# A graph layer and a mixture of experts on one core: quarter slots for an expert's last rows, and columns of A loaded by half blocks

## The chip, the cores and the metric

The kernel runs on one core of a Trainium2 chip. The metric is the device time of one execution in microseconds; the time of a kernel is the median of its runs. One further execution is recorded by the hardware profiler, and all views come from that one.

## What is computed

There are 2048 nodes of 256 features. The layer norm of the rows is gathered over 67,584 weighted edges and summed into the destination rows, with the input and a node vector added. The result `x` goes through a mixture of eight experts: each row is sent to its two best ones.

```python
x = x + gnn(layernorm(x), edge_weight, [src, dst], node_vec1)   # segment sum of w * x[dst] over src
xt = layernorm(x)
logits = xt @ Wr + br                         # Wr: 256 x 8
top_p, top_idx = top_k(softmax(logits), 2);  weights = top_p / sum(top_p)
xn = layernorm(xt);  xe = xn * ln_g[e] + ln_b[e]
h = gelu(xe @ W1[e] + b1[e])                  # 256 x 1024
y = h @ W2[e] + b2[e]                         # 1024 x 256
out = x + sum over the row's two experts of weight * y
```

Everything is float32. 4096 pairs of row and expert have to be computed, about 512 for each expert.

## The kernel before

**Build of A.** The edge sums are matmuls with a dense matrix A (2048 x 2048), which is made on the chip from the sorted edge list. 32 half blocks `n` are made one after another; two of them give one block `cb` of 128 columns. `make_hots` makes one-hot matrices on VectorE (L306, L311, L318), the third part of `hr` on POOL; `make_cols` multiplies them on TensorE with four tiles of 32 columns side by side (L343), ScalarE copies the result to `ar` (L346), SP stores `ar` to `ad` in DRAM (L347) and, after the second half of a block, loads the whole block back as `ac`, in another layout (L350). `dense` (L357) multiplies finished blocks with the normalised rows, VectorE adds the products to `acc` (L364, L367). The last group of four blocks is multiplied after the build.

**Routing.** From `acc` come the second norm, the logits and the two best experts of each row, in two batches (ten blocks of rows, then six). `places` and `enlist` give each pair a spot in its expert's list; the list is kept in tiles of 128. `slots` (L858 to L908) turns the counts into a plan on VectorE: how many whole slots (two tiles, 256 rows) and half slots (one tile, 128 rows) each expert has, and where each slot starts. After it `set_shares` computes the weights of the pairs and SP stores the rows to `xr_d` (L774); SP then reads the plan into registers (L1134) and loads weights.

**Slots.** `load_slot` loads an expert's weights (L932 to L935, 2 MB, on SP) and gathers its rows by index on POOL (L939), into one of seven sets of buffers. `head` transposes the rows (L978), scales them (L987) and forms the weights; `layer_1` does 16 matmuls with gelu on ScalarE (L1013, L1015), `layer_2` 8 matmuls for each tile (L1027), VectorE weighs the result into `ys` (L1030, two buffers), and POOL adds it to `y_d` in DRAM by index (`put_y`, L1035). Stores of one slot are declared free of order among themselves; a store waits for those of other slots.

Ten whole slots always run (three of them early, on the first batch). `halves[0]` and `halves[1]` are loaded at u = 4 and 5, the two final slots at u = 7 and 8. Then come two nests of Ifs on counts from the plan: further whole slots, and after them half slots, as many as there are; with this input four and two. At the end SP copies `y_d` to `out` (L1180) as soon as all stores have landed, while TensorE works on the two final slots; these gather what the copy has for their rows (`so_far`), add it to their bias, and write to `out` (`put_out`, L1048).

The order on TensorE, VectorE, ScalarE and SP is as written; only POOL's is chosen by the scheduler.

## Time and profile before

| what | us |
|---|---|
| median of 3 runs (501.56 to 506.0) | 503.91 |
| the profiled execution | 508.05 |
| its span, first to last instruction | 506.3 |
| TensorE busy | 459.8 (91%) |
| VectorE busy | 273.1 (54%) |
| matmuls of layer 1 (L1013), 576 records | 121.3 |
| matmuls of layer 2 (L1027), 544 records | 121.0 |
| matmuls of the edge sums (L357), 512 records | 126.3 |

A float32 matmul is two records. 576 records of layer 1 are 18 slots of 32; 544 of layer 2 are 34 tiles of 16. Busy times are unions of a group's spans. In lines of the timeline the columns are start, duration, engine, line, operation, tiles written and read, shapes and count, and in brackets the idle time before and what ended it. In the table by stage each engine has its busy microseconds, then come TensorE's granted clock (1.00 is full), the busy share of the DMA engines, and GB/s.

### The profile page before, as it was taken

The numbers are of one execution on the slowest core, as the hardware profiler recorded it, in microseconds if no ns is written. First come the engines' busy times: TensorE is split into PE (matmuls) and PEld (weight loads), VectorE is DVE, ScalarE is ACT, GpSimd is POOL, SyncE is SP. The second block draws the span as 40 slices with busy tenths as digits, with TensorE's granted clock in tenths as the row PEclk, the third lists the DMA queues.
The fourth block names the chain that finished last, engine by engine and source line by source line (L and its number), as shares of the span: only waits on it lengthen the run. The fifth ranks groups of instructions, "written<-read, shape, count | busy, mean of one in ns | idle before, by whom it ended". The sixth has DMA issues, their size and how long they took to land.

```text
span 506.3 us, 12113 instructions
## 1 busy us (share of the span) xinstructions
PE 459.8 (91%) x4996; PEld 394.4 (78%) x4996; DVE 273.1 (54%) x621; ACT 183.8 (36%) x422; POOL 192.7 (38%) x158
## 2 busy tenths in 40 slices
PE   4876599898979999899999899999999999999993
PEld 3775478687758878788888788888888888888882
DVE  7999999999969971317837232323232312212111
ACT  2478524144214210028483323332243433333320
POOL 3477655544533330000142444443452444322231
PEclk9575679899979999999999999999999999999998
DMA  6128678796777667953513997997999677226420
GB/s 214 53 76 246 203 223 269 230 236 186 203 216 221 210 178 239 344 189 105 179 54 84 303 333 214 361 356 210 334 360 309 169 210 210 36 40 204 140 92 31
DMA packets 84356, 102.15 MB, mean 202 GB/s; under 512 B 8240, under 2 KB 74656, under 8 KB 82176
## 3 DMA queue, kind: packets, MB, share of 16 engines
q1 hardware_dynamic: 74832, 86.26, 53.5%
q0 software_dynamic: 7984, 13.91, 11.9%
q10 hardware_dynamic: 1472, 1.06, 0.7%
q8 instruction: 44, 0.72, 0.6%
q14 instruction: 24, 0.20, 0.1%
HBM read 75.18 MB, written 28.14 MB: 204 GB/s over the span
## 4 chain that ended last, share of the span: by engine, by line
PE 35%; DMA 13%; issue 3%; DVE 1%; SPq 0%; ACT 0%; POOL 0%; POOLq 0%; DVEq 0%
PE py L1027 16%; PE ph L1013 15%; DMA xs<-xr_d,to_i 8%; DMA y_d<-ys,to_i 2%; DMA out<-y_d 2%; PE px L978 1%; PE px L834 1%; PE py L357 1%; DMA so_far<-out,to_i 1%; DMA out<-ys,to_i 0%; SPq L1180 0%; POOL out L1048 0%; POOLq L1209 0%; ACT L1015 0%; DVE pick L957 0%
## 5 line engine op out<-in xcount | busy, mean ns | idle before, releaser
L357 PE MATMUL py<-xn_sb,ac 128*128 128x264 f32 x512 | 126.3, 404 | 1.8 <-DVEq L569 1.4
L1013 PE MATMUL ph<-xeT,w 128*128 128x256 f32 (+1 forms) x576 | 121.3, 368 | 2.4 <-PEq L1167 1.7
L1027 PE MATMUL py<-w,hT 128*128 128x256 f32 x544 | 121.0, 379 | 0.0
L1013 PEld LDWEIGHTS ph<-xeT,w 128*128 128x128 f32 x576 | 104.4, 190 | 16.5 <-issue 3.0
L357 PEld LDWEIGHTS py<-xn_sb,ac 128*128 128x128 f32 x512 | 98.5, 197 | 21.7 <-issue 2.2
L1027 PEld LDWEIGHTS py<-w,hT 128*128 128x128 f32 x544 | 101.9, 190 | 12.9
L1015 ACT ACTIVATE hT<-ph,ec 128x256 f32<-128x256 f32 (+1 forms) x144 | 66.2, 462 | 117.6 <-PE ph L1013 60.8
L1035 POOL DMA_INDIRECT y_d<-ys,to_i x30 | 48.5, 1616 | 119.3 <-DVE ys L1030 88.5
L318 POOL TENSOR_TENSOR hr<-eq,w 128x1024 bf16<-128x1024 bf16 x32 | 61.2, 1912 | 81.6 <-DVE hr L318 66.1
L343 PE MATMUL pa<-hl,hr 128*32 128x128 bf16 x3072 | 58.4, 237 | 21.6 <-POOL hr L318 10.8
L343 PEld LDWEIGHTS <-hr 128*32 128x32 bf16 x3072 | 50.0, 106 | 32.6 <-issue 14.0
L306 DVE TENSOR_TENSOR hl<-k,iota_t 128x4096 bf16<-128x4096 bf16 x32 | 72.9, 2278 | 0.0
L987 DVE TENSOR_SCALAR xeT<-px,ec 128x256 f32<-128x256 f32 (+1 forms) x38 | 18.4, 526 | 79.8 <-PE px L978 79.0
L939 POOL DMA_INDIRECT xs<-xr_d,to_i x39 | 40.5, 1038 | 54.2 <-DVE z L702 41.9
L346 ACT COPY ar<-pa 128x512 f32<-128x512 f32 x64 | 36.5, 584 | 59.8 <-PE pa L343 53.6
L1030 DVE SCALAR_TENSOR_TENSOR ys<-py,wt,b2w 128x256 f32<-128x256 f32 x34 | 16.4, 484 | 72.7 <-PE py L1027 61.3
L364 DVE TENSOR_TENSOR acc<-acc,py 128x528 f32<-128x528 f32 x32 | 22.3, 701 | 35.3 <-PE py L357 35.3
L318 DVE TENSOR_TENSOR hr<-eq,w 128x2048 bf16<-128x2048 bf16 x32 | 39.1, 1223 | 0.6
L1002 ACT ACTIVATE b2w<-b,wt 128x256 f32<-128x256 f32 x36 | 16.3, 500 | 34.0 <-DVE wt L1000 32.4
L311 DVE TENSOR_TENSOR eq<-k,iota_t 128x1024 bf16<-128x1024 bf16 x32 | 21.8, 680 | 0.0
L670 ACT ACTIVATE sq<-acc,less_m 128x256 f32<-128x256 f32 x16 | 8.0, 499 | 32.6 <-DVE acc L364 32.6
L296 ACT CAST w<-r 128x256 bf16<-128x256 f32 x16 | 6.5, 405 | 25.0 <-DVE r L295 25.0
(196 smaller groups left out, 303.0 us busy)
## 6 DMA issues: line engine op xcount, KB each, us to landing
w<-in_L_ffn_W SPq DMA_DIRECT2D x40, 1024.0 KB, 9.2
ad<-ar SPq DMA_DIRECT2D x32, 512.0 KB, 8.7
ac<-ad SPq DMA_DIRECT2D x16, 1024.0 KB, 5.9
b<-in_L_ffn_b SPq DMA_DIRECT2D x20, 128.0 KB, 9.8
out<-y_d SPq DMA_DIRECT2D x4, 512.0 KB, 6.3
xr_d<-rec SPq DMA_DIRECT2D x1, 1300.0 KB
y_d<-acc SPq DMA_DIRECT2D x1, 1280.0 KB, 5.1
acc<-in_x SPq DMA_DIRECT2D x2, 512.0 KB, 7.6
```

The costliest lines, as they stand in the source:

```text
L306: nc.vector.tensor_tensor(hl.rearrange("p g (n t) -> p g n t", t=2), two(k2[:, 0], g, P), pair(P), OP.is_equal)
L311: nc.vector.tensor_tensor(eq.rearrange("p g (n t) -> p g n t", t=2), two(k2[:, 1], g, RK), pair(RK), OP.is_equal)
L318: return engine.tensor_tensor(hr[:, i0:i1].rearrange("p i g (n t) -> p (i g) n t", t=2), eq[:, None, :, :].to_broadcast([P, i1 - i0, GH, RK]),
L343: nc.tensor.matmul(pa[j * RK:(j + 1) * RK, m, :], hr[:, i, g, :], hl[:, g, :], start=(i == 0), stop=(i == 2), tile_position=(0, j * RK))
L346: nc.scalar.copy(ar[:, m0:m0 + 4, :], pa)
L357: nc.tensor.matmul(pa[:, i, :DX], acs[c][:, b + i, :], xn_sb[:, c, :], start=(c == cbs[0]), stop=(c == cbs[-1]))
L364: nc.vector.tensor_add(acc[:, b:b + 2, :], acc[:, b:b + 2, :], pa[:, :, :DX])
L939: nc.gpsimd.indirect_dma_start(out=(sets[s.set][0] if into is None else into)[:, t, :], out_offset=None, in_=(xr_d if rows is None else ro ...
L1013: nc.tensor.matmul(ph, w1[:, k, c * P:(c + 1) * P], xeT[:, k, :], start=(k == 0), stop=(k == KD - 1))
L1015: nc.scalar.activation(hT[:, c, :s.n * P], ph, AF.Gelu, bias=ec[:, c:c + 1], scale=1.0)
L1027: nc.tensor.matmul(py, hT[:, c, t * P:(t + 1) * P], w2[:, c, :], start=(c == 0), stop=(c == KH - 1))
L1035: st = nc.gpsimd.indirect_dma_start(out=y_d[:, :], out_offset=bass.IndirectOffsetOnAxis(ap=tos[s.to][:, t:t + 1], axis=0), in_=ys, in_offs ...
```

## The change

An expert with an odd number of tiles whose last tile holds 1 to 32 rows no longer gets a half slot for it: up to two such experts get a quarter slot, run inside the loop of the whole slots. `few_e` and `few_t` hold its expert and tile, found in `slots`. In a quarter slot the 32 rows are the stationary operand, and the hidden units are split over four column tiles of 32; `fold` (32 columns out of a fourfold identity) sums the four partial results. Its five steps `turn`, `first`, `turn_h`, `second` and `total` are hung between matmuls of the slots u = 7 to 9. The quarter slots always run; without such an expert they work on spare rows. The half slots that remain run ahead of the conditional whole slots, and `halves[0]` is no longer loaded early. In the build, each half block gets its own buffer `ad` in DRAM and is loaded back by itself, after the store of the next half block has been issued.

```diff
@@ -83,6 +83,10 @@
+    NQ, QR = 2, 32
+    QW = P // QR
...
@@ -144,7 +148,10 @@
     tile_0 = consts.tile([P, TT, NU], F32, name="tile_0")
-    slot_i = consts.tile([1, NU + 2], I32, name="slot_i")
+    slot_i = consts.tile([1, NU + 2 + NQ], I32, name="slot_i")
+    few_e = consts.tile([P, NQ], F32, name="few_e")
+    few_t = consts.tile([P, NQ], F32, name="few_t")
+    fold = consts.tile([P, QR], F32, name="fold")
     xr_d = dram.tile([N + TS, RW], F32, name="xr_d")
...
@@ -329,10 +336,8 @@
-        cb, h = n // 2, n % 2
-        if h == 0:
-            ads[cb] = dram.tile([P, NB, P], F32, name="ad", bufs=4)
-        ad_v = ads[cb].rearrange("(m j) b r -> (j b) m r", m=GB // QP)
+        ads[n] = dram.tile([P // 2, NB, P], F32, name="ad", bufs=6)
+        ad_v = ads[n].rearrange("(m j) b r -> (j b) m r", m=GH // QP)
         ar = rowsp.tile([P, GH // QP, P], F32, name="ar")
...
@@ -344,10 +349,14 @@
             nc.scalar.copy(ar[:, m0:m0 + 4, :], pa)
-        nc.sync.dma_start(ad_v[:, h * GH // QP:(h + 1) * GH // QP, :], ar)
-        if h == 1:
-            acs[cb] = pool_of[cb].tile([P, NB, P], F32, name="ac")
-            nc.sync.dma_start(acs[cb], ads[cb])
+        nc.sync.dma_start(ad_v, ar)
+        for k in ([n - 1] if n > 0 else []) + ([n] if n == 2 * NB - 1 else []):
+            cb, h = k // 2, k % 2
+            if h == 0:
+                acs[cb] = pool_of[cb].tile([P, NB, P], F32, name="ac")
+            nc.sync.dma_start(acs[cb][h * P // 2:(h + 1) * P // 2], ads.pop(k))
...
@@ -657,8 +667,8 @@
     final = [Slot(FIRST - EARLY, TT, 3, AHEAD + 2, 2), Slot(FIRST - EARLY + 1, TT, 6, AHEAD + 6, 0)]
-    halves = [Slot(NF + i, 1, 4 + i if i < 2 else i % 3, AHEAD + 3 + i % 3, 3 + i % 2)
-              for i in range(NE)]
+    halves = [Slot(NF + i, 1, 4 + i % 2, AHEAD + 3 + i % 3, 3 + i % 2) for i in range(NE)]
+    few = [Slot(i, 1, 4 + i, AHEAD + 3 + i, 3 + i) for i in range(NQ)]
     with tc.manual_schedule(engines=ALL - {ET.Pool}):
...
@@ -858,10 +868,15 @@
             nc.vector.tensor_tensor(tiles_i, ps, over, OP.add)
+            few_i = small_t("few_i", I32)
+            nc.vector.tensor_scalar(few_i, tiles_i, QR.bit_length() - 1, None,
+                                    op0=OP.arith_shift_right)
+            nc.vector.tensor_scalar(few_i, few_i, TS // QR - 1, None, op0=OP.bitwise_and)
             nc.vector.tensor_scalar(tiles_i, tiles_i, 7, None, op0=OP.arith_shift_right)
...
@@ -873,6 +888,25 @@
                                            op1=OP.subtract)
+            is_few = small_t("is_few")
+            nc.vector.tensor_scalar(is_few, few_i, float(P // QR), None, op0=OP.is_equal)
+            n_few = small_t("n_few")
+            nc.vector.tensor_tensor_scan(n_few, ones[:, :NE], is_few, 0.0, op0=OP.mult, op1=OP.add)
+            last = small_t("last")
+            nc.vector.scalar_tensor_tensor(last, iota_p[:, :NE], float(NB), tiles[:, :NE],
+                                           op0=OP.mult, op1=OP.add)
+            for i in range(NQ):
+                it = small_t(f"few{i}")
+                nc.vector.scalar_tensor_tensor(it, n_few, float(i + 1), is_few, op0=OP.is_equal,
+                                               op1=OP.mult)
+                nc.vector.tensor_sub(n_of[:, 1, :], n_of[:, 1, :], it)
+                of_it = small_t(f"of_few{i}")
+                for t, v in ((few_e, iota_p[:, :NE]), (few_t, last)):
+                    nc.vector.scalar_tensor_tensor(of_it, it, 1.0, v, op0=OP.mult, op1=OP.mult,
+                                                   accum_out=t[:, i:i + 1])
+            nc.vector.tensor_scalar(few_t, few_t, -1.0, None, op0=OP.add)
+            nc.vector.tensor_copy(slot_i[:, NU + 2:], few_e[0:1, :])
             upto = route.tile([P, 2, NE], F32, name="upto", bufs=1)
...
@@ -894,7 +928,7 @@
             nc.vector.tensor_copy(slot_i[:, :NU], slot_e[0:1, :])
-            nc.vector.tensor_copy(slot_i[:, NU:], upto[0:1, :, NE - 1])
+            nc.vector.tensor_copy(slot_i[:, NU:NU + 2], upto[0:1, :, NE - 1])
             for i, r in spans:
...
@@ -1056,10 +1090,98 @@
-        def run_slot(s, nxt, more=(), between={}, put=put_y):
+        def load_few(s):
+            e = ds(few_offs[s.i], 1)
+            get_weights(s, W1[e], cols_d[e], W2[e], b2[e])
+            tk = slotp.tile([P, TT], F32, name="tk")[:QR, :1]
+            pick = slotp.tile([P, P], F32, name="pick", bufs=1)[:QR]
+            nc.vector.scalar_tensor_tensor(pick, iota_p[:QR], few_t[:QR, s.i:s.i + 1], lists[:QR],
+                                           op0=OP.is_equal, op1=OP.mult, accum_out=tk)
+            to = slotp.tile([P, TT], F32, name="to")[:QR, :1]
+            nc.vector.scalar_tensor_tensor(to, tk, 0.5, spare_r[:QR, :1], op0=OP.is_lt,
+                                           op1=OP.mult)
+            nc.vector.scalar_tensor_tensor(tos[s.to][:QR, :1], tk, -1.0, to, op0=OP.add,
+                                           op1=OP.max)
+            nc.gpsimd.indirect_dma_start(
+                out=sets[s.set][0][:QR, 0, :],
+                out_offset=None,
+                in_=xr_d[:, :],
+                in_offset=bass.IndirectOffsetOnAxis(ap=tos[s.to][:QR, :1], axis=0),
+            )
+        def few_steps(s):
+            xs, w1, w2, ec, b2r = sets[s.set]
+            xeT, wt, b2w = (t[:QR] if i else t[:, :, :QR] for i, t in enumerate(heads[s.head]))
+            part = lambda j: slice(j * QR, (j + 1) * QR)
+            hs = more_w.tile([P, TS], F32, name=f"hs{s.i}")
+            hT = more_w.tile([P, TT, P], F32, name=f"hT{s.i}")
+            py = more_w.tile([P, D], F32, name=f"py{s.i}")
+            def turn():
+                pt = ps_x.tile([P, KD, TS], F32, name="px")
+                for k in range(KD):
+                    nc.tensor.transpose(pt[:, k, :QR], xs[:QR, 0, k * P:(k + 1) * P],
+                                        ident[:QR, :QR])
+                for k in range(KD):
+                    nc.vector.tensor_scalar(xeT[:, k, :], pt[:, k, :QR], ec[:, KH + k:KH + k + 1],
+                                            ec[:, KH + KD + k:KH + KD + k + 1],
+                                            op0=OP.mult, op1=OP.add)
+                mine = slotp.tile([P, TT, 2], F32, name="mine")[:QR, 0, :]
+                nc.vector.tensor_scalar(mine, xs[:QR, 0, D:D + 2], few_e[:QR, s.i:s.i + 1], None,
+                                        op0=OP.is_equal)
+                wr = slotp.tile([P, TT, 2], F32, name="wr")[:QR, 0, :]
+                nc.vector.tensor_mul(wr, mine, xs[:QR, 0, D + 2:D + 4])
+                nc.vector.tensor_reduce(wt, wr, AX.X, OP.add)
+                nc.scalar.activation(b2w[:, 0, :], b2r[:QR], AF.Copy, scale=wt)
+            def first():
+                ph = ps_h.tile([P, TS], F32, name="ph")
+                for k in range(KD):
+                    for j in range(QW):
+                        nc.tensor.matmul(ph[part(j), :], xeT[:, k, :],
+                                         w1[:, k, j * TS:(j + 1) * TS], start=(k == 0),
+                                         stop=(k == KD - 1), tile_position=(0, j * QR))
+                nc.vector.tensor_copy(hs, ph)
+            def turn_h():
+                pt = ps_h.tile([P, TS], F32, name="ph").rearrange("p (t r) -> p t r", t=TT)
+                for t in range(TT):
+                    nc.tensor.transpose(pt[:, t, :], hs[:, t * P:(t + 1) * P], ident)
+                each = lambda a: a.rearrange("p t (j r) -> p t j r", j=QW)
+                bias = ec[:, :KH].rearrange("p (j t) -> p t j", t=TT)[..., None]
+                nc.vector.tensor_tensor(each(hT), each(pt), bias.to_broadcast([P, TT, QW, QR]),
+                                        OP.add)
+                nc.scalar.activation(hT, hT, AF.Gelu)
+            def second():
+                pa = listed.rearrange("p a b -> p (a b)")
+                for t in range(TT):
+                    for j in range(QW):
+                        nc.tensor.matmul(pa[part(j), :], hT[:, t, part(j)], w2[:, j * TT + t, :],
+                                         start=(t == 0), stop=(t == TT - 1),
+                                         tile_position=(0, j * QR))
+                nc.vector.tensor_copy(py, pa)
+            def total():
+                pa = counts.rearrange("p a b e -> p (a b e)")[:QR, :D]
+                nc.tensor.matmul(pa, fold, py, start=True, stop=True)
+                ys = slotp.tile([P, D], F32, name="ys")[:QR]
+                nc.vector.scalar_tensor_tensor(ys, pa, wt, b2w[:, 0, :], op0=OP.mult, op1=OP.add)
+                nc.gpsimd.indirect_dma_start(
+                    out=y_d[:, :],
+                    out_offset=bass.IndirectOffsetOnAxis(ap=tos[s.to][:QR, :1], axis=0),
+                    in_=ys,
+                    in_offset=None,
+                    compute_op=OP.add,
+                )
+            return turn, first, turn_h, second, total
+        def run_slot(s, nxt, more=(), between={}, put=put_y, between_1={}):
             for m in more:
                 m()
-            hT = layer_1(s)
+            hT = layer_1(s, between_1)
             if nxt is not None:
...
@@ -1135,6 +1257,10 @@
         )
+        _, few_offs = nc.values_load_multi_w_load_instructions(
+            slot_i[0:1, NU + 2:], engines=[mybir.EngineType.SP], min_val=0, max_val=NE - 1,
+            skip_runtime_bounds_check_because="an expert's number, or none",
+        )
         load_slot(whole[EARLY])
...
@@ -1148,15 +1274,40 @@
             nc.vector.memset(t, 0.0)
+        nc.vector.tensor_reduce(fold, ident.rearrange("p (j r) -> p r j", r=QR), AX.X, OP.add)
         for u in range(3, FIRST):
             more = later(load_slot if u + 2 <= FIRST else load_rows, whole[u + 2])
-            more += later(load_slot, *{4: halves[:1], 5: halves[1:2], 7: final[:1], 8: final[1:]}.get(u, []))
-            also = {FIRST - 2: halves[0], FIRST - 1: final[0]}.get(u)
-            run_slot(whole[u], whole[u + 1], more, {1: lambda: head(also)} if also else {})
+            more += later(load_slot, *{7: final[:1], 8: final[1:]}.get(u, []))
+            more += later(load_few, *{4: few[:1], 5: few[1:]}.get(u, []))
+            f = u - (FIRST - 1 - NQ)
+            between, between_1 = {}, {}
+            if 0 <= f < NQ:
+                steps = few_steps(few[f])
+                between[1] = steps[0]
+            if 0 <= f - 1 < NQ:
+                between_1 = {1: ready[1], 5: ready[2]}
+                between[0] = ready[3]
+                between.setdefault(1, lambda: None)
+                t0, t1 = between[1], ready[4]
+                between[1] = lambda t0=t0, t1=t1: (t1(), t0())
+            if u == FIRST - 1:
+                t0 = between.get(1, lambda: None)
+                between[1] = lambda t0=t0: (t0(), head(final[0]))
+            run_slot(whole[u], whole[u + 1], more, between, between_1=between_1)
+            if 0 <= f < NQ:
+                ready = steps
     _, (n_whole, n_half) = nc.values_load_multi_w_load_instructions(
...
     )
+    with ExitStack() as nest:
+        for u, s in enumerate(halves):
+            nest.enter_context(tc.If(n_half > s.i - NF))
+            with tc.manual_schedule(engines=ALL - {ET.Pool}):
+                if u == 0:
+                    load_slot(s)
+                head(s)
+                run_slot(s, None, later(load_slot, *halves[u + 1:u + 2]))
     with ExitStack() as nest:
...
@@ -1164,14 +1315,6 @@
                          + later(load_rows, *whole[u + 2:u + 3]))
-    with ExitStack() as nest:
-        for u, s in enumerate(halves):
-            nest.enter_context(tc.If(n_half > s.i - NF))
-            with tc.manual_schedule(engines=ALL - {ET.Pool}):
-                if u >= 2:
-                    head(s)
-                run_slot(s, halves[1] if u == 0 else None,
-                         later(load_slot, *halves[u + 1:u + 2] * (u > 0)))
...
```

## The prediction

> **What bounds the kernel now.** First the totals and the table by stage, to see which engine has no slack where.
>
> ```profile
> PE 459.8 (91%) x4996; PEld 394.4 (78%) x4996; DVE 273.1 (54%) x621; ACT 183.8 (36%) x422; POOL 192.7 (38%) x158
> core 0: us, PE busy (x) PEld busy (x) DVE busy (x) ACT busy (x) POOL busy (x), PEclk, DMA share, GB/s
> 80.00:120.00 40.00, 37.83 (x871) 30.87 (x862) 39.04 (x60) 15.91 (x41) 19.83 (x14) 0.96 0.78 220
> 290.00:396.00 106.00, 106.00 (x510) 93.42 (x509) 31.22 (x125) 34.93 (x75) 44.75 (x35) 1.00 0.95 305
> 453.00:468.00 15.00, 14.53 (x98) 13.37 (x98) 2.74 (x12) 6.39 (x17) 4.21 (x3) 1.00 0.67 181
> ```
>
> Up to about 190 us, where the columns of A are built, VectorE is full (39.04 of 40 us); from 290 us TensorE is full (106.00 of 106 us). So in the build a microsecond counts if it is VectorE's, and among the slots if it is TensorE's. Then the timeline of TensorE at the end of the slots:
>
> ```profile
> 445.38 7.07 PE L1027 MATMUL py<-w,hT 128*128 128x256 f32 x32
> 453.03 3.83 PE L1013 MATMUL ph<-xeT,w 128*128 128x128 f32 x32 [0.57 <-PEq L1160]
> 456.91 3.62 PE L1027 MATMUL py<-w,hT 128*128 128x256 f32 x16
> 460.37 3.73 PE L1013 MATMUL ph<-xeT,w 128*128 128x128 f32 x32
> 463.94 3.62 PE L1027 MATMUL py<-w,hT 128*128 128x256 f32 x16
> 469.22 7.14 PE L1013 MATMUL ph<-xeT,w 128*128 128x256 f32 x32 [1.66 <-PEq L1167]
> ```
>
> Two half slots run between the last whole slot and the two final ones, with a gap of TensorE's sequencer at each branch out of a nest of Ifs. Working the reference's routing on its inputs gives the experts 544, 509, 506, 482, 502, 510, 536 and 507 rows: the half slots carry the last 32 and 24 rows of experts 0 and 6, both within the change's 32. Third, the one stall among the slots, from the timelines of VectorE, SP, POOL and TensorE:
>
> ```profile
> 268.28 0.16 DVE L864 TENSOR_TENSOR tiles_i<-counts,over 128x8 int32<-128x8 f32 x1
> 272.66 0.22 DVE L908 TENSOR_TENSOR tile<-tile,skipped 128x54 f32<-128x54 f32 x1
> 273.45 0.36 SPq L774 DMA_DIRECT2D xr_d<-rec  x1
> 280.14 1.03 POOL L939 DMA_INDIRECT xs<-xr_d,to_i  x1 [0.30 <-DVE to L961]
> 287.67 0.44 PE L978 MATMUL px<-ident,xs 128*128 128x128 f32 x2 [1.88 <-DMA xs<-xr_d,to_i]
> ```
>
> The planner `slots` (L864 to L908) stands on VectorE ahead of the shares, these ahead of the store of the rows, and that ahead of the gather for `whole[3]`. TensorE waits 1.88 us for that gather, so this chain has no slack.
>
> **What the Trainium skill says.** "TensorE: Matmul & The Clock Gate", Part 3 (Packing small matmuls), says matmuls in different column tiles run concurrently while matmuls still start in program order. The trace agrees: L343 starts in groups of four column tiles, and 96 of them take 1.46 us (166.58 to the next line's 168.04, below), 15 ns each. The same page, Part 1, says the clock halves after an idle window of about 3.4 us; here the table has clock 1.00 at 498 to 502 us, after the last matmul ended at 497.5, and 0.51 at 502 to 506. "Runtime: NRT & Kernel Launch", Instruction fetch mechanics, says a taken branch breaks sequential prefetch; the gaps of 0.57 and 1.66 us above agree in place.
>
> ```profile
> 166.58 1.52 PE L343 MATMUL pa<-hl,hr 128*32 128x128 bf16 x96
> 168.04 2.94 PE L357 MATMUL py<-xn_sb,ac 128*128 128x264 f32 x12
> 92.89 1.07 ACT L346 COPY ar<-pa 128x512 f32<-128x512 f32 x2 [1.45 <-DMA ad<-ar]
> 131.27 0.70 DVE L364 TENSOR_TENSOR acc<-acc,py 128x528 f32<-128x528 f32 x1 [0.80 <-PE py L357]
> ```
>
> **The change, part by part.** The sum is made against the profiled execution: 508.05 us, span 506.3. The median of the runs is 503.91; I carry the difference over to it.
>
> (a) The half slots go. The last whole slot's matmuls end at 452.45. Its branch gap of 0.57 stays, so the finals start at 453.02 instead of 469.22: 16.2 us less on TensorE. But the end also hangs on the last store to `y_d`, the copy to `out`, and the gathers of `so_far`. Before, that store was issued 1.53 us after the last matmul of the slots (467.56 to 469.09); after `whole[13]` it is 0.87 us (452.45 to 453.32). This chain had 0.65 us of slack against TensorE (`b2w` done at 496.33, first `ys` 0.5 us, second `ys` at 497.56). The last two POOL stores stand in series. So I take 15.8 off. The transposes of `halves[0]` at 377.08 go too: 0.2.
>
> (b) Two quarter slots come, on TensorE. Each issues two transposes of 32 rows (`turn`), 8 matmuls of 32 columns by 256 (`first`), two transposes (`turn_h`), 8 such matmuls (`second`) and one of 256 (`total`). A float32 matmul is two records: 32 records of 256 columns take 6.91 us, 216 ns each. Transposes: 4 in 0.44 us. The trace has no column-tiled float32. With no overlap, 8 matmuls take 16 x 0.216 = 3.46 us; with four side by side as at L343, 0.86 plus the 0.18 us that L343 lost against its ideal (estimate: 1.46 less 96 x 53.3 ns / 4, with the page's price of 128 columns), 1.04. But the two records of one matmul use the same column tile, and starts are in order: the second record waits 216 ns, and only the next tile's first record can go beside it. That gives 9 steps of 216 ns, 1.95 us, which I take. Each quarter: 0.12 + 1.95 + 0.22 + 1.95 + 0.43 = 4.7; with some draining 4.8. Two: +9.6 us (6.0 to 15.5).
>
> (c) `slots` gets 15 small VectorE instructions and four accumulator reads ahead of the store. The 13 instructions from 268.28 to 270.33 have a pitch of 0.158 us, dependent ones 0.20, and a read adds 0.12. 15 x 0.16 + 4 x 0.12 = 2.9 us. Beside it: `head(whole[2])` is ready at 278.6 instead of 275.7, when TensorE needs it at 278.50, so nearly free. SP's two more register loads delay the weights of `whole[3]` by 0.3 us more, hidden, since they were issued 16 us ahead of use. The gather moves by the whole amount. POOL may order it ahead of the store that now precedes it and win back 1.3 us. I take +2.7 (1.5 to 4; the upper end if a gap of now 4.6 us halves the clock for a while).
>
> (d) The nest of halves is now jumped over ahead of the conditional whole slots: one gap. Long cover in TensorE's queue gave 0.57, short cover 1.66. There is a layer's second half ahead of it: +0.6 (0 to 1.7). Of the other engines, VectorE has some 10 us to its next urgent work, ScalarE 5.3, and SP runs ahead.
>
> (e) The store of a quarter slot is not exempted from order with the other stores to `y_d`, which need 6.7 us in the median to land. POOL holds it behind the first store of its whole slot and holds the second store behind it. `ys` has two buffers, and a third user now comes in a slot: VectorE's second `ys` waits for the first store. In the slot after the first quarter this blocks VectorE until about 7.5 us after the first tile's matmuls. Picks (1.2 us) stand ahead of the copy of `hs`, done near 9.7. TensorE, with three `ph` buffers, wants that one back near 8.6: +1.2 us (0 to 4). Gathers behind POOL's stores have 10 us to spare.
>
> (f) Half-block loads. SP no longer sits behind a load that waits for its own store: it waited 102.9 us in all for `ad` at L350. What of this reaches VectorE? ScalarE waited three times for `ad` (2.63, 1.45, 1.25 us), delaying TensorE, and soon after VectorE idled 0.95, 0.61 and 0.80 us for `py`. At the first, TensorE also waited for `ac`, of which only half is now late. So -1.7 (-2.4 to +0.5, the latter for 16 more issues on SP). The last columns landed near 204 us and are needed at 209: no gain there.
>
> Loads of quarter slots stand where those of halves stood, with the same four weight DMAs and a gather of fewer rows; the reduction for `fold` falls in VectorE's idle time. Nothing for these.
>
> Sum: -15.8 - 0.2 + 9.6 + 2.7 + 0.6 + 1.2 - 1.7 = -3.6 us. Profiled execution 504.4; median 503.9 - 3.6 = 500.3.
>
> **The rivals.**
> 1. Column tiles in float32 overlap fully: the hardware lets the records of four tiles go side by side. For: L343. Against: the order of records within a matmul. Four groups at 1.04 instead of 1.95 take off 3.6: 496.7 us.
> 2. They don't overlap at all. For: no float32 tile has run here, and each streams other columns of weights. 4 x (3.46 - 1.95) = +6.0: 506.3 us, slower than before. It decides when a group takes over 1.95 + 3.6 / 4 = 2.85 us; below that, the change still gains.
> 3. The order of the stores is exposed: landings near the maximum of 9.3 us push POOL's gathers for `whole[12]` past their 10 us of slack, +4: 504.3 us. Against: DMA load falls from 0.95 to 0.53 after 396 us.
> 4. The change doesn't do what it says: expert 0 has just 32 rows left, and one more would send it to a half slot, whose weights are now loaded only inside its If. 7.3 us of matmuls and some 9.2 us to landing: 517 us. Against: the routing worked above.
>
> **How the numbers follow.** Forecast 0.52, rivals 0.25, 0.12, 0.07, 0.04. About 1% (5 us) is what a measurement of this kernel tells from no change. With a spread of some 2.7 us, the forecast puts 0.30 beyond -1%, rival 1 0.87; together 0.38. Slower: a quarter of rival 2, rival 4 and tails, 0.09. Range: 495.0 (rival 1 with some luck in (c) and (f)) to 506.5 (rival 2).
>
> **What would show it.** Right: no 128-wide L1013 after the loop, and the finals under 1 us after the last whole slot; the groups of `first` and `second` near 1.95 us; a stall near 4.6 us before `px` of `whole[3]`; no wait of `ar` for `ad`. Wrong: groups near 1.0 or 3.5 us; a stall of `ph` on the copy of `hs` above 2 us; 128-wide matmuls still there.

## Result, and the profile after

On one chip the kernel after took 499.24 us (median of 4 runs, 497.61 to 500.84), the kernel before 504.40 us (median of 4, 501.56 to 506.0). The ratio is 0.9881, 95% interval 0.9845 to 0.9918: 1.2% faster. The profiled execution after is 498.29 us with a span of 496.5; that of before, 508.05, was above its kernel's median, so the difference of the two spans, 9.8 us, overstates the gain. It is used below for where time goes, not for how much.

The totals of the kernel after, and its table by stage (stretch, length, busy time of TensorE, its weight loads, VectorE, ScalarE and GpSimd, then clock, DMA share, GB/s):

```profile
PE 450.9 (91%) x4972; PEld 381.3 (77%) x4972; DVE 276.1 (56%) x643; ACT 178.4 (36%) x408; POOL 195.3 (39%) x157
```

```profile
80.00:120.00 40.00, 38.98 (x884) 31.96 (x885) 39.72 (x57) 15.17 (x41) 21.88 (x15) 1.00 0.91 234
290.00:396.00 106.00, 106.00 (x550) 89.51 (x548) 32.02 (x131) 34.92 (x75) 43.95 (x35) 1.00 0.91 290
453.00:468.00 15.00, 14.45 (x70) 12.44 (x69) 2.38 (x8) 4.70 (x10) 4.45 (x4) 1.00 0.28 56
```

The bounds are the same: VectorE in the build, TensorE among the slots. TensorE is busy 8.9 us less. Its timeline, first from the first quarter slot, then the two jumps out of the nests:

```profile
365.35 1.07 PE L1142 MATMUL ph<-w,xeT 128*32 128x256 f32 x16
366.35 3.72 PE L1047 MATMUL ph<-xeT,w 128*128 128x256 f32 x16
...
373.25 1.07 PE L1161 MATMUL listed<-w,hT 128*32 128x256 f32 x16
374.25 3.72 PE L1061 MATMUL py<-w,hT 128*128 128x256 f32 x16
377.90 0.62 PE L1168 MATMUL counts<-py,fold 128*32 128x256 f32 x2
...
401.63 7.14 PE L1047 MATMUL ph<-xeT,w 128*128 128x256 f32 x32 [1.21 <-PEq L1303]
...
459.68 7.14 PE L1047 MATMUL ph<-xeT,w 128*128 128x256 f32 x32 [0.55 <-PEq L1311]
```

No matmul of a half slot is left; a group of eight column-tiled matmuls takes 1.00 us from its start to the next line's. The stall before `whole[3]`, from the timelines of SP, GpSimd and TensorE (the gather has one transfer for each of the slot's two tiles; `px` is its transposed rows):

```profile
271.22 0.36 SPq L784 DMA_DIRECT2D xr_d<-rec  x1
274.67 1.56 POOL L1069 DMA_INDIRECT y_d<-ys,to_i  x1 [11.05 <-DVE ys L1064]
276.54 1.07 POOL L973 DMA_INDIRECT xs<-xr_d,to_i  x1 [0.30 <-issue]
277.91 1.04 POOL L973 DMA_INDIRECT xs<-xr_d,to_i  x1 [0.30 <-issue]
283.17 0.41 PE L1012 MATMUL px<-ident,xs 128*128 128x128 f32 x2 [1.92 <-DMA xs<-xr_d,to_i]
284.14 0.69 PE L1012 MATMUL px<-ident,xs 128*128 128x128 f32 x2 [0.56 <-DMA xs<-xr_d,to_i]
284.62 8.24 PE L1061 MATMUL py<-w,hT 128*128 128x256 f32 x32
```

TensorE waits twice for the gather, and the layer after it takes 8.24 us instead of 7.07: its granted clock was 0.50 from 284 to 286 us. The gather's indices were there at 272.5 us, and the rows that it reads, stored by SP at 271.22, had landed 4.0 us later, at about 275.2. On GpSimd it stands behind a store that waits for `ys`, so it starts at 276.54, some 1.3 us after its rows.

To split the time I take two parts of each profiled execution: the build and first routing, from the start to the first matmul of `counts` (L751 before, L761 after), and the rest, from there to the end of the span.

| kernel | build | rest | ratio to before |
|---|---|---|---|
| before | 234.73 | 271.55 | 1 |
| after | 230.41 | 266.11 | 0.9881 |
| after, second chip | 230.49 | 265.81 | 0.9899 |
| A by whole blocks, quarters | 243.80 | 266.07 | 1.0023 |
| loads alone, no quarters | 230.88 | 270.03 | 0.9928 |
| quarter steps left out | 232.35 | 262.96 | 0.9799 |
| old order of the nests | 228.19 | 273.08 | 1.0011 |
| shares ahead | 231.54 | 261.84 | 0.9763 |
| shares ahead, second chip | 229.70 | 261.64 | 0.9803 |
| loads and shares, no quarters | 231.12 | 269.11 | 0.9924 |
| shares ahead, whole blocks | 237.28 | 261.63 | 0.9952 |
| shares ahead, loaded at once | 278.63 | 261.33 | 1.0645 |
| shares ahead, loaded two later | 234.35 | 261.73 | 0.9804 |

Read the column "rest" first: the five kernels with quarters and shares ahead agree within about 0.5 us, the three with the slots of the kernel after within 0.3. It is less steady where TensorE waits for the gather of `whole[3]`: the kernel before and that with the loads alone are alike behind the build and differ by 1.5 us, 1.1 of it in this wait (16.36 and 15.26 us from the first matmul of `whole[2]` to that of `whole[3]`). The build is less steady still; the times of a kernel, too, spread over some 7 us in the kernel before (502.88 to 510.41 in one lot of 11 runs).

### The profile page after: what moved, and what is told of

It is laid out like the page before. It is cut to its first block, busy times and chain, and to the rows that moved or that the text cites. A ratio compares the mean times of both kernels' runs of the same rounds, so it can differ in the third digit from the quotient of the medians.

```text
span 496.5 us, 12069 instructions
## 1 busy us (share of the span) xinstructions
PE 450.9 (91%) x4972; PEld 381.3 (77%) x4972; DVE 276.1 (56%) x643; ACT 178.4 (36%) x408; POOL 195.3 (39%) x157
## 5 line engine op out<-in xcount | busy, mean ns | idle before, releaser
L366 PE MATMUL py<-xn_sb,ac 128*128 128x264 f32 x512 | 124.0, 398 | 6.3 <-issue 3.6
L366 PEld LDWEIGHTS py<-xn_sb,ac 128*128 128x128 f32 x512 | 96.8, 193 | 25.6 <-issue 7.6
L1047 PE MATMUL ph<-xeT,w 128*128 128x256 f32 x512 | 114.7, 380 | 1.9 <-PEq L1303 1.2
L1061 PE MATMUL py<-w,hT 128*128 128x256 f32 x512 | 115.5, 383 | 0.0
L1047 PEld LDWEIGHTS ph<-xeT,w 128*128 128x128 f32 x512 | 96.7, 190 | 16.5 <-issue 1.7
L1061 PEld LDWEIGHTS py<-w,hT 128*128 128x128 f32 x512 | 96.9, 192 | 13.3 <-issue 0.8
L1049 ACT ACTIVATE hT<-ph,ec 128x256 f32<-128x256 f32 x128 | 60.4, 473 | 105.0 <-PE ph L1047 58.5
L1069 POOL DMA_INDIRECT y_d<-ys,to_i x28 | 45.4, 1622 | 101.8 <-DVE ys L1064 69.3
L973 POOL DMA_INDIRECT xs<-xr_d,to_i x36 | 37.5, 1041 | 60.2 <-DVE z L712 40.2
L1021 DVE TENSOR_SCALAR xeT<-px,ec 128x256 f32<-128x256 f32 x34 | 16.9, 539 | 66.6 <-PE px L1012 65.8
L373 DVE TENSOR_TENSOR acc<-acc,py 128x528 f32<-128x528 f32 x32 | 22.2, 700 | 29.9 <-PE py L366 29.9
```

Source lines behind the costliest of these rows:

```text
L366: nc.tensor.matmul(pa[:, i, :DX], acs[c][:, b + i, :], xn_sb[:, c, :], start=(c == cbs[0]), stop=(c == cbs[-1]))
L373: nc.vector.tensor_add(acc[:, b:b + 2, :], acc[:, b:b + 2, :], pa[:, :, :DX])
L973: nc.gpsimd.indirect_dma_start(out=(sets[s.set][0] if into is None else into)[:, t, :], out_offset=None, in_=(xr_d if rows is None else ro ...
L1047: nc.tensor.matmul(ph, w1[:, k, c * P:(c + 1) * P], xeT[:, k, :], start=(k == 0), stop=(k == KD - 1))
L1049: nc.scalar.activation(hT[:, c, :s.n * P], ph, AF.Gelu, bias=ec[:, c:c + 1], scale=1.0)
L1061: nc.tensor.matmul(py, hT[:, c, t * P:(t + 1) * P], w2[:, c, :], start=(c == 0), stop=(c == KH - 1))
```

## Experiments

**The two parts apart.** First the kernel after with `make_cols` as before:

```diff
...
-        nc.sync.dma_start(ad_v, ar)
-        for k in ([n - 1] if n > 0 else []) + ([n] if n == 2 * NB - 1 else []):
...
+        nc.sync.dma_start(ad_v[:, h * GH // QP:(h + 1) * GH // QP, :], ar)
+        if h == 1:
+            acs[cb] = pool_of[cb].tile([P, NB, P], F32, name="ac")
+            nc.sync.dma_start(acs[cb], ads[cb])
```

> The changed kernel with make_cols as it was before: whole blocks loaded back, the store of the next half behind them; the quarter slots stay. Theory 1: the 4.3 us by which the build is shorter in the trace of the changed kernel come from the half-block loads; then this one takes 499.2 + 4.3 = 503.5 us, about as long as before. Theory 2: most of the 4.3 us is spread between executions (the profiled one of before took 508.05 at a median of 504.4), and the loads give at most the 1.7 us forecast; then this one takes 499.5 to 501 us, and ScalarE again waits some 5 us for ad in all.

It took 506.89 us, 1.0023 (0.9967 to 1.0079) of the kernel before, longer than either theory had it. Then the opposite, the kernel before with the new `make_cols` and nothing else:

> The kernel before with only the new make_cols: half blocks loaded behind the next store, no quarter slots. Theory 1: 504.4 - 4.3 = 500.1 us. Theory 2: 502.5 to 505 us, within 0.4% of before. In both the waits of ScalarE for ad go and SP's waits at the loads fall from 103 us to some 20.

502.66 us, 0.9928 (0.9879 to 0.9977), as theory 2 has it. With its loads undone the whole change is worth nothing, though the rest is as short as in the kernel after (266.07 us). So the loads are needed for the gain; but the loads alone give only 0.7% of the 1.0 to 1.2%. The two don't add up, and a later run returns to that.

**Quarters without their work.** The steps of the quarter slots are not issued, so the last 32 and 24 rows of experts 0 and 6 are left out:

```diff
-                between[1] = steps[0]
...
-                between_1 = {1: ready[1], 5: ready[2]}
-                between[0] = ready[3]
...
```

> The changed kernel with the steps of the quarter slots left out (the last 32 and 24 rows of experts 0 and 6 are not computed); planner, loads of weights and rows and everything else stay. If the quarters lie fully on TensorE's path, the slots u = 7 to 9 fall by the 7.5 us read from the two traces, and the time from 499.2 to 491.8. Rival: part of it was hidden behind a wait that now shows (rows or weights that come late, stores to y_d): 493 to 496 us. The late gather for whole[12] and the 0.24 us stall of px at it should go.

496.82 us, 0.9799 (0.9743 to 0.9855); both theories had less. That is some 4 us less than the kernel after by the ratios, and some 3 us less in the rest, where the quarters' own matmuls take 7.5. The jump over the nest of halves eats 3.2 us of the difference; the matmul here, then the sequencer's branch (count, duration in ns as lowest/median/highest, first and last start) here and in the kernel after:

```profile
398.38 8.83 PE L1047 MATMUL ph<-xeT,w 128*128 128x256 f32 x32 [2.68 <-PEq L1298]
```

```profile
L1298 PEldq COMPARE_BRANCH  x1: 5315/5315/5315, 392.5 to 392.5; - x1
```

```profile
L1303 PEldq COMPARE_BRANCH  x1: 3915/3915/3915, 397.3 to 397.3; - x1
```

The gap is 2.68 us instead of 1.21, and layer 1 takes 8.83 instead of 7.14, with a granted clock of 0.50 at 400 to 402 us. In both kernels the branch begins some 3.1 us before TensorE has finished what it holds; here it takes 5.3 us instead of 3.9, and why is not shown. A further 0.7 us is the wait for the gather of `whole[3]`, longer in this profile.

**Column tiles in float32.** In quarter 0 the same eight matmuls of `first` are issued tile by tile; in quarter 1 all eight first go through a single column tile, as extra work:

```diff
...
+                if s.i == 1:
+                    for j in range(QW):
+                        for k in range(KD):
+                            nc.tensor.matmul(ph[part(0), :], xeT[:, k, :],
+                                            w1[:, k, j * TS:(j + 1) * TS], start=(k == 0),
+                                            stop=(k == KD - 1),
+                                            tile_position=(0, 0))
+                order = [(k, j) for k in range(KD) for j in range(QW)]
+                if s.i == 0:
+                    order = [(k, j) for j in range(QW) for k in range(KD)]
...
```

> The changed kernel with first of quarter 0 issued tile by tile (the two matmuls of a column tile one after the other), and first of quarter 1 preceded by eight further matmuls that all use column tile 0. Theory A, the records of one matmul need not be neighbours and any four tiles in the window overlap: the tile-by-tile group takes the 1.00 us measured in the changed kernel. Theory B, matmuls start in program order and the overlap came only from the order with tiles innermost: two neighbours on one tile halve the overlap, 1.8 to 2.0 us, or 2.8 if all four records of a tile are serial. Eight matmuls on one tile: 16 x 0.216 = 3.46 us without any overlap. TensorE's path grows by 3.5 to 5.3 us.

From TensorE's timeline:

```profile
368.28 1.09 PE L1150 MATMUL ph<-w,xeT 128*32 128x256 f32 x16
369.30 3.72 PE L1047 MATMUL ph<-xeT,w 128*128 128x256 f32 x16
...
386.15 3.42 PE L1143 MATMUL ph<-w,xeT 128*32 128x256 f32 x15
389.20 0.42 PE L1150 MATMUL ph<-w,xeT 128*32 128x256 f32 x3
389.41 0.38 PE L1143 MATMUL ph<-w,xeT 128*32 128x256 f32 x1
```

Tile by tile, 1.02 us; on one tile, sixteen records one behind the other, the last of them (389.41) starting 3.26 us after the first. So the 1.00 us is true overlap of four tiles, and of the two orders of issue neither is faster. Three records of later matmuls even start at 389.20, ahead of the last record on the single tile. One run of this kernel took 506.6 us; it is longer than the kernel after for other reasons too (`px` waited 2.10 and 1.32 us for the gather), so its time is not read.

**The place of the jump.** The two nests in the old order, whole slots first:

> The kernel after with its two nests of Ifs at the end in the old order: nest of the whole slots first, then that of the halves; nothing else differs and all is computed. Theory 1 (the place of the jump decides what it costs): the 1.2 us gap that TensorE shows at the start of whole[10]'s layers goes, GpSimd's late gather for whole[12] (8.7 us idle, px 0.24 us late) goes, u=9's start to whole[10]'s start falls by 1 to 1.5 us and whole[10] to whole[12] by 0.3 to 0.5 us; a gap of 1.5 to 2 us stands before the first matmul of the finals instead, where no engine has work queued, against 0.55 in the kernel after: within 1 us of it in all, some 498 to 501 where the kernel after has 499.2. Theory 2 (a jump costs the same wherever it stands, and the nests' order is free): the gap moves with it, no difference over 0.3 us in the sum of both places.

504.89 us, 1.0011 (0.9986 to 1.0035): both theories were far off. TensorE's timeline:

```profile
449.34 7.07 PE L1061 MATMUL py<-w,hT 128*128 128x256 f32 x32
461.63 9.94 PE L1047 MATMUL ph<-xeT,w 128*128 128x256 f32 x32 [5.22 <-PEq L1311]
```

The branches of its sequencer at the lines of the two nests (count, duration in ns as lowest/median/highest, first and last start):

```profile
L1303 PEldq COMPARE_BRANCH  x6: 65/69/3425, 396.3 to 456.6; - x6
L1311 PEldq COMPARE_BRANCH  x1: 4462/4462/4462, 456.9 to 456.9; - x1
```

With this input no half slots are left, so both nests are left by a jump, one right after the other: the first takes 3.43 us, from 452.39, and is hidden behind queued matmuls; the second begins at 456.86, when TensorE has run dry, and its 4.46 us are bare. Layer 1 of the first final slot then starts at a clock of 0.50 (462 to 466 us, and 0.68 in the two after) and takes 9.94 us, 2.8 more. In the kernel after, the two jumps last 3.92 and 3.71 us and stand apart, each begun 3 to 4 us before TensorE has finished what it holds: 1.21 and 0.55 us show. In the rest the old order costs 7.0 us, but 1.2 of it is a longer wait for the gather of `whole[3]` in this profile (19.72 us from `whole[2]` to `whole[3]` instead of 18.52). So the swap of two nests, which the change makes in passing, is worth some 6 us, and the ratios say the same.

**Shares ahead of the planner.** To free the gather of `whole[3]`:

```diff
-        slots(last_b["all"])
         set_shares(last_b)
+        slots(last_b["all"])
```

> The kernel after with set_shares of the last batch (three DVE operations and the xr_d store) called before the slots' planner instead of after it; all is computed. In its program order GpSimd's gathers for whole[3] then stand ahead of the y_d stores of whole[1], where in the kernel after they stand behind one that waits for ys until 274.7 us. Theory 1 (the planner's 2.1 us more on DVE hurts through the xr_d store and the order on GpSimd, not through the planner's end itself): the gathers go out some 3 to 3.8 us earlier relative to whole[2]'s layers, as soon as to_i is there (272.4 us in the kernel after), px of whole[3] no longer waits (2.5 us in the kernel after), the granted clock stays at 1.0 after it (1.2 us), and whole[2] to whole[3] falls from about 18.5-20 us to 15: 3 to 4 us off the whole, a ratio to the kernel before of about 0.981. Theory 2 (the gathers are bound by to_i behind the longer planner on DVE): px stalls by 1.5 us or more still, less than 1.5 us off the whole.

493.20 us, 0.9763 (0.9718 to 0.9808). GpSimd and TensorE:

```profile
273.93 1.08 POOL L973 DMA_INDIRECT xs<-xr_d,to_i  x1 [9.18 <-DVE to_i L997]
275.31 1.04 POOL L973 DMA_INDIRECT xs<-xr_d,to_i  x1 [0.30 <-issue]
276.66 1.67 POOL L1069 DMA_INDIRECT y_d<-ys,to_i  x1 [0.31 <-DVE pick L991]
...
282.22 0.60 PE L1012 MATMUL px<-ident,xs 128*128 128x128 f32 x4
282.66 7.07 PE L1061 MATMUL py<-w,hT 128*128 128x256 f32 x32
```

Relative to `whole[2]`'s first matmul the gather goes out 3.7 us earlier (1.38 us before it instead of 2.36 after it), ahead of the stores; `px` doesn't wait, layer 2 takes 7.07 us again. `whole[2]` to `whole[3]` is 14.26 us, 18.52 in the kernel after. The planner is as long as in the kernel after; its 2 us more on VectorE are hidden.

Two things move together in this run: SP stores the rows at 265.74, ahead of the planner, and GpSimd has the gather ahead of the stores. By the trace of the kernel after, the new order alone could have brought the gather forward by the 1.3 us since its rows had landed, and earlier rows alone by nothing, as long as it stood behind the store of `ys`. So the 3.7 us need both; neither was run alone. The rest is 4.3 us shorter, which is the 18.52 less 14.26. The medians on this chip differ by 7.4 us; what goes beyond the 4.3 lies in the build, which this edit doesn't touch.

**The kernel after on the same chip,** for comparison:

> The kernel after unchanged, for comparison on the same chip. Every theory: a ratio to the kernel before of 0.984 to 0.992. With the ratio of the kernel without its two quarter slots (0.980) it prices the quarters at 2 to 6 us; eight matmuls of a quarter in 1.00 us, px of whole[3] waiting 2 to 3.5 us, whole[2] to whole[3] 18.5 to 20.5 us.

500.60 us, 0.9899 (0.9852 to 0.9946), as expected. And the same step in a kernel without quarters:

> The kernel before (half slots, no quarters, short planner) with the new order of A's loads, as in the earlier run of the loads alone (ratio 0.993), and set_shares of the last batch called before the slots' planner. Theory 1 (quarters are worth their 16.2 us less 7.5 us in their layers, less the jump and the planner, about 4 to 6 us, once the gathers stand right): px of whole[3] waited 1.9 us in the kernel before and does not here, 0.5 to 2 us off the loads-alone time, ratio 0.989 to 0.992, and the kernel after with the same order of shares is 4 to 6 us faster than this one. Theory 2 (the quarters pay nothing and all gain is the loads'): this one is within 1.5 us of the kernel after with the same order.

501.79 us, 0.9924 (0.9897 to 0.9950). Against the kernel with quarters and shares ahead, the rest is 7.3 us longer: once the gather is not in the way, quarters for halves pay 7.3 us, more than the 4 to 6 expected. With it in the way they pay 3.9 (270.03 to 266.11), or 5.4 from the kernel before.

**Which half of the loads matters.** On the version with the shares ahead, each half block is loaded right after its own store:

```diff
-        for k in ([n - 1] if n > 0 else []) + ([n] if n == 2 * NB - 1 else []):
+        for k in [n]:
```

> The kernel with the shares ahead of the planner, and each half block of A loaded back right after its own store is issued, not after the next one; all is computed. It splits the loads' gain into the half blocks and the place behind the next store. Theory 1 (the order carries it: SP stands at the load until its own store has landed, and the next stores of ar stand behind it on SP): SP waits for ad over 100 us again, ScalarE waits for ad when it writes ar, the build (start to the first matmul of counts) ends 3 us or more later, 235 to 244 us instead of 228 to 232.4, ratio to the kernel before 0.985 to 0.995 against 0.976. Theory 2 (the smaller blocks carry it: half the bytes are late at a time): the build ends by 232.5 us and the time is within 2 us of the kernel with the shares ahead.

540.15 us, 1.0645 (1.0592 to 1.0698): theory 1, and far more of it than expected. The longest waits of SP up to 255 us and of ScalarE from 24 to 230 us (line, what was waited for, us in total, times, longest):

```profile
SPq L359 <- DMA ad<-ar: 169.4, 31, 6.7
```

```profile
ACT ar L351 <- DMA ad<-ar: 102.4, 20, 7.1
```

SP's in the kernel before, with whole blocks, and in the kernel after:

```profile
SPq L350 <- DMA ad<-ar: 102.9, 19, 9.3
```

```profile
SPq L359 <- DMA ad<-ar: 22.2, 9, 3.6
```

With each load right behind its store, SP stands at 31 of 32 loads until the store before it has landed, and the next store of `ar` stands behind that load. One store and one wait for its landing now follow each other for each half block, ScalarE runs out of the three `ar` buffers, and the build is 47 us longer. Small blocks alone would have been a large loss. Two stores later instead of one:

> The same kernel with each half block loaded two stores later instead of one (eight buffers ad instead of six). Theory 1 (the wait of SP is gone with one store between, what is left is VectorE's own work): build within 1.5 us of that of one store later, time within 2 us, ratio 0.974 to 0.980; SP's wait for ad falls from 22 to under 10 us. Theory 2 (SP's remaining 22 us still delay the build): 1 to 3 us faster.

495.98 us, 0.9804 (0.9772 to 0.9836); the wait of SP at the loads for `ad`, 18.3 us with one store between, falls to 1.1 us, and nothing is won. The version with one store between, on the same chip:

> The kernel with the shares ahead of the planner, unchanged, for comparison on the same chip: ratio to the kernel before 0.971 to 0.981, build end 228 to 232.5 us, no wait at px of whole[3], whole[2] to whole[3] 14.3 to 15 us.

495.27 us, 0.9803 (0.9752 to 0.9855).

**Whole blocks again, with the shares ahead:**

> Quarter slots with the shares ahead of the planner, but A's columns loaded by whole blocks as in the kernel before; all is computed. The kernel with whole-block loads and the shares behind the planner gave 1.002 (0.997 to 1.008), that with half-block loads and the shares ahead 0.976 to 0.980. Theory 1 (the parts add up: loads 3.6 us as in the kernel that has them alone, shares some 4.5 us as between the kernel after and that with the shares ahead): ratio 0.983 to 0.990, 498 to 502 us, no wait at px of whole[3], build end 234 to 240 us. Theory 2 (with whole-block loads the build itself lengthens when the quarters are there, as the first build end of 243.8 us hints, and the shares don't mend it): ratio 0.992 or more, build end 241 us or later.

502.27 us, 0.9952 (0.9923 to 0.9981), theory 2 by the ratio, though not by the profiled build. The rest is 261.63 us, so the loss is all in the build. For the median builds I subtract the rest and the 1.77 us between span and time from each median (an estimate): 231 to 233 us for the kernel before over its five lots, 230 to 233 for all kernels with half-block loads one or two stores later, 239 for both with whole blocks and quarters. In the kernel before, half-block loads take off some 0.6 to 2.2 us of the build (with the loads alone it is 502.66 - 1.77 - 270.03 = 230.9, and 233.1 for the kernel before on that chip); in the kernel after they are worth 6 to 9. These estimates lean on the rest of one profile each; with the 270.03 us of the loads alone the builds of the kernel before would be 1.5 us longer. On every engine the build of that last kernel issues the same instructions in the same order as the kernel before; why whole blocks cost some 6 to 8 us more there stays open.

## Why the prediction was right, step by step

The forecast of 500.3 us is 1.1 us from the median. Its sum was -3.6 us; the medians say -5.2. Between the two profiled executions the rest gives -5.4 us where (a) to (e) had -1.9. The steps, from the starts of layers in both:

- **(a)** -16.0 forecast. The halves' 16.19 us went, 0.26 at the end and 0.22 of transposes: -16.7. Right, and the finals follow the last whole slot with a gap of 0.55 us, as stated.
- **(b)** +9.6 forecast, measured 7.5. The term that failed is the 1.95 us for a group of eight: "the second record waits 216 ns, and only the next tile's first record can go beside it". The groups took 1.00 us, which is rival 1's mechanism, and 1.02 us when issued tile by tile, so the order of starts, on which the term leaned, does not hold them up. The Trainium skill says in "TensorE: Matmul & The Clock Gate", Part 3, that column tiles run at once; the trace now shows it for float32, where both records of a matmul overlap with those of the other tiles. What the sum lacked is small: after a group of 32-column matmuls the next group is up to 0.2 us longer (eight matmuls of `py` 3.65 us from 374.25 to 377.90, where sixteen take 6.91). A quarter costs 3.7 us instead of 4.8, so rival 1's 3.6 us became 2.1.
- **(c)** +2.7 forecast, +2.2 between these two profiles. The planner grew by 2.1 us on VectorE (263.95 to 270.64, where before it was 268.28 to 272.88), 2.9 forecast, so this term was too large. "The gather moves by the whole amount" was right. GpSimd before:

```profile
276.90 1.55 POOL L1035 DMA_INDIRECT y_d<-ys,to_i  x1 [8.96 <-DVE ys L1030]
278.76 1.08 POOL L939 DMA_INDIRECT xs<-xr_d,to_i  x1 [0.30 <-issue]
```

The gather's two transfers start 0.26 and 1.64 us after `whole[2]`'s first matmul (278.50) before, and 2.36 and 3.73 us after it (274.18) in the kernel after: 2.1 later, in the same order on GpSimd. But the link was another than the prediction's chain has it. The rows had landed 1.3 us ahead of the gather in both kernels (before at about 277.5: 273.45 and 4.0 us); what the gather stood behind was GpSimd's store, and `ys`, for which that waits, comes behind the planner on VectorE as well. The stall was 2.48 us in two pieces, not 4.6, because the planner grew by less and because the planner grew by less and because the second transfer, which TensorE waited for before, landed in 6.2 us instead of 7.5: the sum had carried the time to land over unchanged. So layer 2 starts 1.0 us later, and the clock costs a further 1.2, which the prediction had only at its upper end. The skill's Part 1 on that page names an idle window of about 3.4 us; here two waits of 1.92 and 0.56 us with a little work between them were enough, and in the run without quarters one gap of 2.68 us. Over all kernels with the planner ahead `whole[2]` to `whole[3]` took 18.5 to 20.8 us, and with the short planner 16.36 and 15.26, so other pairs of profiles would put (c) anywhere from 2.2 to 5.6 us. Free of the stall it is 14.26.

- **(d)** +0.6 forecast, 1.21 of gap and 0.33 in the slots after it, 1.5 in all. The second part was not foreseen: GpSimd's gather for `whole[12]` went out at 419.05 after 8.68 us idle, and `px` was late. "Runtime: NRT & Kernel Launch", Instruction fetch mechanics, names the broken prefetch at a taken branch. The runs show the duration, 3.3 to 5.3 us of TensorE's sequencer for each taken jump; that the fetch is what takes it no run here shows.
- **(e)** +1.2 forecast, 0 on TensorE. VectorE did wait, 2.58 us at its longest, for a store to `y_d`, but the copy of `hs` was done in time and no `ph` waited.
- **(f)** -1.7 forecast. The two profiled builds differ by 4.3 us, mostly because before's execution was a long one. By medians it is -2.2 in the kernel with the loads alone, -0.6 in that with loads and shares, and about 0 between before and after, each uncertain by the 1.5 us named above; the forecast can't be refused. The trigger it named is confirmed: with whole blocks SP waits for `ad` at the load, with a store between hardly (102.9 and 22.2 us in all).

So the total is right partly by luck: 2.1 us too much in (b) and 1.2 in (e) stand against 0.9 too little in (d), with 1.2 more gained in (a) and (c), and a (f) that came to less. Rival 1 had the mechanism of (b) right and its size wrong; rivals 2 and 4 didn't happen. The gather that rival 3 named, for `whole[12]`, was late, by 0.24 us at `px`; but it follows GpSimd's own branch at 409.2, and with the nests in the old order it goes out at 407.88, so the jump held it and not the stores.

The version with the shares ahead of the planner beats both kernels: 0.9763 and 0.9803 of the kernel before on two chips, with 0.9899 for the kernel after on the first of them.

## What to carry to other kernels

A taken jump costs as much as the work queued ahead of it fails to cover: put a nest that is likely to be jumped over behind a long queue of matmuls, and don't put two such jumps in a row. A load that waits for a store on the same queue also holds every later store there, so put at least one independent transfer between them before making the blocks smaller. When a chain gets longer, follow it through the queue that issues its last transfer: here the planner's 2.1 us reached the gather through a store that stands in front of it, and the stall went only when the rows were stored ahead of the planner and the gather was issued ahead of that store.

## What was not expected of the hardware

- Eight float32 matmuls of 32 columns by 256 over four column tiles took 1.00 and 1.02 us in two orders of issue; on one tile the last record started 3.26 us after the first.
- TensorE's sequencer spent 3.3 to 5.3 us in a taken branch, and in the kernel after began it 3 to 4 us before TensorE had finished its queued work; between 0.55 and 5.22 us of it showed.
- After 5.22 us without work TensorE's granted clock was 0.50 for at least 4 us, and one layer took 9.94 us instead of 7.14. After a gap of 2.68 us it was 0.50 as well; after one of 1.88 us, in the kernel before, it stayed at 1.00.
